# GroupNorm, attention and projection over 16 images: group statistics on VectorE, v's bias at v or at the attention's output, the accumulator as two tiles, and another place for raw projection weights

## The chip, the cores and the metric

The kernel runs on one core of a Trainium2 chip. The metric is the device time in microseconds (us) of one execution, given as the median of several runs. All times in this section of the document are of the kernel before the change.

## The reference

Sixteen images x of 512 channels and 32x32 positions (N = 1024), all in fp32, go through one layer:

```python
xg = x.reshape(b, NUM_GROUPS, -1)                    # 8 groups of 64 channels
mu = jnp.mean(xg, axis=-1, keepdims=True)
var = jnp.var(xg, axis=-1, keepdims=True)
xn = ((xg - mu) * jax.lax.rsqrt(var + EPS)).reshape(b, c, h, w)
xn = xn * norm_gamma[:, None, None] + norm_beta[:, None, None]
qkv = jnp.einsum('oc,bchw->bohw', qkv_w, xn) + qkv_b[:, None, None]
...
attn = jax.nn.softmax(jnp.einsum('bhnd,bhmd->bhnm', q, k) * scale, axis=-1)
out = jnp.einsum('bhnm,bhmd->bhnd', attn, v)         # 4 heads of 128 channels
...
out = jnp.einsum('oc,bchw->bohw', proj_w, out) + proj_b[:, None, None]
return x + out
```

As the softmax's weights of a position sum to one, v's bias may be added to v, or to the attention's output behind the division, or be carried through proj_w into the projection's bias.

## The kernel before

Channels lie in the 128 partitions, so an image is four tiles of 128x1024 (c = 0 to 3), and a group of 64 channels is half the partitions of one tile. The attention sets the pace. One step s is (image b, head h, key block j of 8); 512 steps make the run. In each step and for each half of 512 query positions PE (TensorE) computes scores s (`scores`, L844), ACT (ScalarE) the exp into p (L850), and PE, one step later, adds v times p to the accumulator po (`weighted_sum`, L912). DVE (VectorE) keeps the running sum of the exps, tot (L858), from which `denominators` and `divide` make the division. At j = 7 ACT copies po to the head's output o (L919).

All other work is cut into units that are dealt out into these steps by `plan_head` (L1059), and run between the two halves' attention matmuls (`run`, L1237). In head 0 an image makes q and k of its own heads 2 and 3; in head 1 the projection of the image before, and loading, statistics and normalising of the next; in head 2 the next image's q and k of heads 0 and 1; in head 3 its v (`v_groups`, L754). In image 0 the weights are prepared as well.

The three projections are two-level fast products of seven (`two_levels`, with the matmuls at L604): each inner product sums in PSUM (tags x and y of ps_a, two banks each); ACT copies partial results (L484), DVE adds them (L628), and the outer sums follow on DVE (L677). The weights' sums are made once in image 0 on DVE from raw blocks that SP's DMA queue loads (`stage_blocks` L367, `group_weights` L390), stored in DRAM (kept, L441) and later loaded from there (L406). For v, `finish` (L758) adds two outer parts (vt, L766), transposes in blocks (vu, L769) and sends the result through DRAM (L777, L782).

Statistics: `stats_chunk` (L256) lets ACT sum x and the squared deviations of each channel, for each of the four tiles. `stats_group` (L270) then averages over the channels of a group with two matmuls against avg, a matrix of 1/64: pm (L83) of the means and pv (L88) of the variances, with small DVE operations at L82 to L89, a power on POOL (GpSimd, L90), and sc, t, sh (L76, L100, L102). `normalise` (L293) applies scale and shift, mostly on ACT. In image 0's own opening the same steps are written out by hand.

v's bias: `bias_of_v` (L929), in head 1 of image 0, multiplies it with proj_w by 32 matmuls of one column (pb, L935; 4x4 blocks, fp32 matmuls are recorded twice) and adds it to the projection's bias.

The order on each engine is set by a scheduler that follows the order of the program. `tc.high_priority(URGENT)` lets an instruction go ahead of others of its engine, `tc.issue_after(ins)` puts one behind another, and `keep_in_program_order` pins it. The scheduler adds the semaphores. A matmul that overwrites a tile waits for the readers of that tile. po is one tile of two banks, [128, 1024]:

```python
if j == 0 and half == 0:
    po[b, h] = ps_o.tile([P, N], F32, tag="o", name=f"po_{b}_{h}")
...
last_eviction[b] = nc.scalar.copy(os_[b, h][:, i], po[b, h][:, i])
```

Of the kernel before, what the change touches and what calls it, by code (L numbers as in the profile page):

```python
# [186 lines left out]
def fast_path(ctx, tc, x, sources, out, consts, flag, dims):  # L187
# [35 lines left out]
    ones = one.tile([BLK, 1], F32, name="ones")  # L223
    xs, xb, vs, qs, ks, os_, ob = {}, {}, {}, {}, {}, {}, {}
# [23 lines left out]
    nc.vector.memset(neghalf, -0.5)  # L248
    for t, src in (
        (gamma_sb, gamma), (beta_sb, beta), (qkb_sb, qk_b), (vb_sb, v_b), (projb_sb, proj_b)  # L250
    ):
        nc.gpsimd.dma_start(t, src)
# [3 lines left out]
    def stats_chunk(b, c):  # L256
        if c == 0:
            mvs[b] = gn.tile([P, NCC, 2], F32, tag="mv", name=f"mv_{b}")

        junk = lpool.tile([P, N], F32, tag="tt", name=f"junk_{b}_{c}")  # L260
        sums = gn.tile([P, 3], F32, tag="st", name=f"sums_{b}_{c}")
        nc.scalar.activation(junk, xs[b, c], AF.Identity, accum_out=sums[:, 0:1])
        nc.scalar.mul(mvs[b][:, c, 0:1], sums[:, 0:1], 1.0 / N)
        nc.scalar.mul(sums[:, 1:2], sums[:, 0:1], -1.0 / N)
        nc.scalar.activation(
            junk, xs[b, c], AF.Square, bias=sums[:, 1:2], accum_out=sums[:, 2:3]
        )
        nc.scalar.mul(mvs[b][:, c, 1:2], sums[:, 2:3], 1.0 / N)

    def stats_group(b):  # L270


        g = []

        def part(n, first, last):
            if not g:
                g.extend(norm.group_steps(mvs[b]))
            with tc.issue_after(added[b - 1, 1, n].ins), tc.high_priority(URGENT):
                for step in g[first:last]:
                    step()  # L280

        def scale():
            n = 4 if b > 1 else 3
            part(n, 9, 10)
            with tc.issue_after(added[b - 1, 1, n].ins), tc.high_priority(URGENT):
                mu, sc = norm.result
                sh = norm.shift(mu, sc)
            for c in range(NCC):
                scaled[b, c] = sc, sh, c

        return [lambda: part(2, 0, 6), lambda: part(3, 6, 9), scale]
# [75 lines left out]
    def stage_blocks(site):  # L367
# [4 lines left out]
        if site in ("proj", "v"):  # L372
# [381 lines left out]
    def v_groups(b):  # L754
# [3 lines left out]
        def finish(which, h, a, c):  # L758
# [7 lines left out]
            nc.vector.tensor_add(t, a, c)  # L766
# [74 lines left out]
    def scores(s, half):  # L841
# [7 lines left out]
        with tc.high_priority(URGENT):  # L849
            exps[s] = nc.scalar.activation(ps[s][:, ts(half, HALF)], sc, AF.Exp, scale=SCALE)  # L850
        i = ts(half, HALF) if s == steps - 1 else ds(0, N)
# [55 lines left out]
    def weighted_sum(s, half):  # L907
        b, h, j = where(s)
        if j == 0 and half == 0:
            po[b, h] = ps_o.tile([P, N], F32, tag="o", name=f"po_{b}_{h}")  # L910
        i = ts(half, HALF)
        nc.tensor.matmul(  # L912
            po[b, h][:, i], v_block(b, h, j), ps[s][:, i],
            start=(j == 0), stop=(j == NB - 1),
        )
        if j == NB - 1:
            if (b, h) not in os_:
                os_[b, h] = opool.tile([P, N], F32, tag="o", name=f"o_{b}_{h}")
            last_eviction[b] = nc.scalar.copy(os_[b, h][:, i], po[b, h][:, i])  # L919

    def divide(b, h):
        nc.vector.tensor_mul(os_[b, h], os_[b, h], rinv.pop((b, h)))

# [4 lines left out]

    def bias_of_v(o):  # L929

        acc = ps_a.tile([P, HALF], F32, tag="y", name=f"pb_{o}")
        half, r = divmod(o, 2)
        for c in range(NCC):
            block = stage["proj"][f"a{half + 1}{c // KC + 1}"]
            nc.tensor.matmul(  # L935
                acc[:, 0:1], block[:, ts(r * KC + c % KC, P)], vb_sb[:, c : c + 1],
                start=(c == 0), stop=(c == NCC - 1),
            )
        nc.vector.tensor_add(
            projb_sb[:, o : o + 1], projb_sb[:, o : o + 1], acc[:, 0:1]  # L940
        )
# [116 lines left out]

    def plan_head(b, h):  # L1059
# [9 lines left out]
        elif h == 1:  # L1069
# [4 lines left out]
            else:  # L1074
                plan[0].append(lambda: load_x(b + 1))
                spread(plan, [lambda c=c: stats_chunk(b + 1, c) for c in range(NCC)], 2, 4)
                sums, power, scale = stats_group(b + 1)
                if b == 0:

                    plan[4] += [sums, power, scale]  # L1080
                else:
                    plan[4].insert(0, sums)
                    plan[4].insert((len(plan[4]) + 1) // 2, power)
                    plan[5].insert(0, scale)
                for r in range(2):
                    plan[5 + r] += [

                        lambda c=c, half=half: normalise(b + 1, c, half, b > 0 or c % 2 == 1)
                        for c in range(KC * r, KC * r + KC) for half in range(NH2)
                    ]  # L1090
                plan[6].append(lambda: x_sums(b + 1, (1,)))
            if b == 0:
                for g in range(len(OUTER)):
                    plan[g // 2].append(lambda g=g: kept_group("v", g))
                    plan[NB // 2 - 1 + g].append(lambda g=g: kept_group("proj", g))
                plan[2].append(lambda: stage_blocks("proj"))
                spread(plan, [lambda o=o: bias_of_v(o) for o in range(NCC)], 3, 5)
# [111 lines left out]

    plan = []  # L1210
    for s in range(steps + 1):
# [12 lines left out]
        for half in range(NH2):  # L1224
            if s < steps:
# [4 lines left out]
                if half == 1 and j == 4 and s > NB:  # L1230

                    with tc.issue_after(added[b, h, 4].ins):
                        divide(*where(s - NB)[:2])
            if s > 0:
                weighted_sum(s - 1, half)
            n = (len(units) + 1) // 2
            run(units[half * n : (half + 1) * n])  # L1237
        if s > 0:
            del ps[s - 1]
# [7 lines left out]
def general_path(ctx, tc, x, sources, out, consts, dims):  # L1247
# [26 lines left out]
    with tc.For_i(0, B, 1) as b:  # L1274
# [16 lines left out]
        for h in range(HEADS):  # L1291
# [9 lines left out]
            for qb in range(NB):  # L1301
# [27 lines left out]
                nc.scalar.copy(o[h][:, ts(qb, P)], acc[:, :P])  # L1329
# [46 lines left out]
```

## Time and profile before

| what | value |
|---|---|
| median of 3 runs | 3169.19 us (3167.69 to 3172.65) |
| profiled execution, its own time | 3171.08 us |
| its span | 3169.3 us |
| granted TensorE clock | 1.0 |
| mean DMA rate | 166 GB/s |
| L83 pm, 34 records | 4.9 us busy |
| L88 pv, 34 records | 6.5 us busy |
| L935 pb, 32 records | 3.8 us busy |
| L766 vt, 120 instructions | 90 of them 711 ns mean, 30 of them 712 |

How to read it. Times in the timeline count from the span's start. A row gives the start, the length, the engine, the line of the kernel, the operation, output <- inputs, tile shape and, behind x, the number of instructions joined in the row; in brackets stand idle time ahead of it and what ended it. Matmuls are pipelined: a row's length runs past the start of the next, so that the distance from start to start is what an instruction takes of PE. "PEld" is the loading of weights into PE, and "SPq" the DMA queue of SP. "Idle" in a group's row is the idle time of that engine just before its instructions.

### The profile page before, as it was taken

Reading aid. Unit: us, or ns where it says so; the run is one execution under the profiler, and the core shown is the slowest. Engines: PE = TensorE matmul, PEld = TensorE weight load, DVE = VectorE, ACT = ScalarE, POOL = GpSimd, SP = SyncE. Lnnn points to the kernel's source line nnn. Section 1 sums busy time; section 2 is a strip of 40 time slices with the busy share of each in tenths; the row PEclk is TensorE's granted clock in tenths of the full one; section 3 lists DMA queues with packets and bytes.
Section 4 is the critical chain, followed back from the end, with each engine's and each line's share of the span. In section 5 each row is a group of like instructions: output and inputs, shape, how many; then the busy total and the mean of one; then the engine's idle time right before and its main releaser. Section 6 shows DMA issues by size and latency. Waiting matters only on the chain.

```text
span 3169.3 us, 34227 instructions
## 1 busy us (share of the span) xinstructions
PE 3156.8 (100%) x10502; PEld 2188.2 (69%) x10502; DVE 2635.8 (83%) x4642; ACT 1438.3 (45%) x2711; POOL 516.3 (16%) x896
## 2 busy tenths in 40 slices
PE   9999999999999999999999999999999999999999
PEld 7566676677776776767767667677676776766664
DVE  9878879788897888878888787987879978788785
ACT  3535435354353443535435454453534545344333
POOL 0011221111211112211122111222012221122200
PEclk9999999999999999999999999999999999999999
DMA  5554554545545555454554545555455564555531
GB/s 176 186 190 154 187 173 152 173 152 194 168 164 163 155 184 176 167 165 144 193 173 159 170 144 192 167 174 171 144 177 170 176 187 133 178 158 187 180 119 48
DMA packets 210668, 524.83 MB, mean 166 GB/s; under 512 B 32176, under 2 KB 65456, under 8 KB 210480
## 3 DMA queue, kind: packets, MB, share of 16 engines
q1 hardware_dynamic: 133088, 282.39, 28.6%
q0 software_dynamic: 64000, 204.54, 19.3%
q10 hardware_dynamic: 13392, 35.66, 3.5%
q8 instruction: 86, 1.41, 0.2%
q14 instruction: 102, 0.84, 0.1%
HBM read 389.30 MB, written 133.17 MB: 165 GB/s over the span
## 4 chain that ended last, share of the span: by engine, by line
PE 96%; DVE 2%; DMA 1%; issue 0%; SPq 0%; POOL 0%; ACT 0%; ACTq 0%; DVEq 0%
PE s L844 27%; PE po L912 27%; PE qk_x L604 12%; PE qk_y L604 9%; PE pp_x L604 6%; PE v_x L604 6%; PE v_y L604 4%; PE pp_y L604 4%; PE lx L999 0%; DVE qk_t L572 0%; DMA x<-in_x 0%; PE ly L999 0%; DVE tot L858 0%; DVE qk_r L628 0%; DVE qk L712 0%
## 5 line engine op out<-in xcount | busy, mean ns | idle before, releaser
L912 PE MATMUL po<-p,v 128*128 128x512 f32 x2048 | 1049.4, 594 | 0.7 <-ACT p L850 0.7
L850 ACT ACTIVATE p<-s 128x512 f32<-128x512 f32 x1024 | 610.6, 596 | 963.7 <-PE s L844 960.0
L844 PE MATMUL s<-qk,qk 128*128 128x512 f32 x2048 | 1047.4, 593 | 0.3 <-DVE qk L712 0.3
L912 PEld LDWEIGHTS po<-p,v 128*128 128x128 f32 x2048 | 603.6, 302 | 322.7 <-issue 214.5
L858 DVE TENSOR_TENSOR tot<-tot,p 128x1024 f32<-128x1024 f32 x385 | 470.2, 1221 | 158.1 <-ACT p L850 156.1
L844 PEld LDWEIGHTS s<-qk,qk 128*128 128x128 f32 x2048 | 387.7, 190 | 88.6 <-issue 29.9
L604 PEld LDWEIGHTS qk_x<-qk_t,w 128*128 128x128 f32 x1344 | 251.8, 190 | 166.1 <-issue 75.3
L604 PE MATMUL qk_x<-qk_t,w 128*128 128x256 f32 x1344 | 356.3, 382 | 0.1
L484 ACT COPY qk_u<-qk_x 128x512 f32<-128x512 f32 (+1 forms) x256 | 136.2, 532 | 229.6 <-PE qk_x L604 229.6
L777 POOL DMA_DIRECT2D vd<-vu x120 | 66.6, 556 | 902.9 <-DVE vu L769 899.5
L628 DVE TENSOR_TENSOR qk_r<-qk_y,qk_u 128x512 f32<-128x512 f32 (+1 forms) x256 | 158.1, 618 | 34.7 <-ACT qk_u L484 21.5
L578 POOL DMA_DIRECT2D kept_t<-qk_t x240 | 129.3, 540 | 278.5 <-DVE qk_t L572 212.0
L604 PEld LDWEIGHTS pp_x<-pp_t,w_proj 128*128 128x128 f32 x630 | 117.2, 190 | 74.7 <-issue 32.3
L628 DVE TENSOR_TENSOR v_r<-v_y,v_u 128x512 f32<-128x512 f32 (+1 forms) x120 | 76.6, 638 | 110.5 <-ACT v_u L484 80.3
L604 PE MATMUL pp_x<-pp_t,w_proj 128*128 128x256 f32 x630 | 167.8, 383 | 0.0
L782 POOL DMA_DIRECT2D v<-vd x240 | 140.5, 592 | 166.6 <-DMA vd<-vu 63.3
L604 PE MATMUL v_x<-v_t,w_v 128*128 128x256 f32 x630 | 166.6, 381 | 0.0
L828 POOL DMA_DIRECT2D out_y<-y x120 | 65.9, 550 | 603.3 <-DVE y L827 601.5
L604 PEld LDWEIGHTS v_x<-v_t,w_v 128*128 128x128 f32 x630 | 118.4, 190 | 55.3 <-issue 19.1
L604 PE MATMUL qk_y<-x,w 128*128 128x256 f32 x512 | 142.2, 379 | 1.5 <-DVE qk_r L628 1.5
L769 DVE STREAM_TRANSPOSE vu<-vt 128x512 f32<-128x512 f32 x120 | 135.7, 1131 | 4.5 <-DMA vd<-vu 4.4
L712 DVE SCALAR_TENSOR_TENSOR qk<-qk_r,qkb_sb,qk_r 128x512 f32<-128x512 f32 x192 | 137.7, 744 | 1.6
(203 smaller groups left out, 4420.0 us busy)
## 6 DMA issues: line engine op xcount, KB each, us to landing
w<-kept SPq DMA_DIRECT2D x90, 512.0 KB, 3.7
kept_t<-qk_t POOLq DMA_DIRECT2D x180, 256.0 KB, 3.5
v_t<-kept_t SPq DMA_DIRECT2D x180, 256.0 KB, 2.9
w<-kept SPq DMA_DIRECT2D x90, 384.0 KB, 3.3
rinv<-row ACTq DMA_DIRECT2D x63, 512.0 KB, 5.0
x<-in_x POOLq DMA_DIRECT2D x60, 512.0 KB, 4.6
vd<-vu POOLq DMA_DIRECT2D x120, 256.0 KB, 3.0
v<-vd POOLq DMA_DIRECT2D x240, 128.0 KB, 4.2
```

Source lines behind the costliest of these rows:

```text
L484: nc.scalar.copy(t[n][:, :width], t["x"][:, :width])
L578: nc.gpsimd.dma_start(t, to)
L604: nc.tensor.matmul(acc[:, ts(i, Q)], have["w"][t][:, i, slot, :], inner(i, bn), start=(first and i == 0), stop=True, skip_group_check=True,)
L628: nc.vector.tensor_add(dst, view(a), view(c))
L712: nc.vector.scalar_tensor_tensor(st[b, h][:, ts(half, HALF)], a, qkb_sb[:, i : i + 1], c, ALU.add, ALU.add)
L769: nc.vector.transpose(u.rearrange("p (q i j) -> p j q i", q=n, i=BLK), t.rearrange("p (j q i) -> p j q i", q=n, i=BLK),)
L777: nc.gpsimd.dma_start(rows[which][ts(h, P), :], u)
L782: nc.gpsimd.dma_start(vs[b, pair][ts(q, BLK), half].rearrange("m h (k i) j -> m (h k) (i j)", k=n), rows[which].rearrange("(k m) (q e) -> ...
L844: nc.tensor.matmul(sc, ks[b, h][:, ts(j, P)], qs[b, h][:, ts(half, HALF)], start=True, stop=True)
L850: exps[s] = nc.scalar.activation(ps[s][:, ts(half, HALF)], sc, AF.Exp, scale=SCALE)
L858: added[b, h, j] = nc.vector.tensor_add(tot[b, h][:, i], tot[b, h][:, i], ps[s][:, i])
L912: nc.tensor.matmul(po[b, h][:, i], v_block(b, h, j), ps[s][:, i], start=(j == 0), stop=(j == NB - 1),)
```

## The change

Four things.

1. *Statistics of images 1 to 15.* ACT writes each tile's means and sums of squared deviations into the columns of a table of [128, 2, 32], which POOL sets to zero once (one small ACT multiplication a tile less). DVE sets the counts, transposes the table in 32x32 blocks, copies each quadrant's block beside that of its neighbour (32 partitions each), and one bn_aggr joins the 64 triples of count, mean and sum. POOL's power follows, on one column; then DVE transposes a broadcast of the result back, and makes sc, t and sh. The first part (`gather`) is issued behind the running sum of j = 3 in step 4, the second (`scale`) behind that of j = 4 in step 5 (in image 0: both in step 4, behind j = 3). No matmul is left; the opening of image 0 keeps its two pairs.
2. *v's bias.* `bias_of_v`'s matmuls go. From image 1 on the add at vt is a scalar_tensor_tensor that adds the bias too. Image 0's v comes out of another path and stays without it; there ACT adds the bias to each head's output, four activations of 128x1024, behind the exps of steps 18, 26, 34 and 38. The general path, which does not run here, adds it at its copy.
3. *po* is two tiles, one for each half.
4. *Image 0's head 1.* The raw blocks of proj_w and their sums lie in the tiles r0 and r1, which otherwise hold outer results, and are loaded in step 0 (before: in tiles of y and ot2, in step 2); the kept sums of proj are made one step earlier; image 1's odd tiles are normalised behind an exp. In images 1 to 14 the running sum of head 1, j = 6 is issued behind the units of its step.

```diff
@@ -223,2 +223,3 @@
     ones = one.tile([BLK, 1], F32, name="ones")
+    table = one.tile([P, 2, BLK], F32, name="table")
     xs, xb, vs, qs, ks, os_, ob = {}, {}, {}, {}, {}, {}, {}
@@ -248,2 +249,3 @@
     nc.vector.memset(neghalf, -0.5)
+    nc.gpsimd.memset(table, 0.0)
     for t, src in (
@@ -256,5 +258,6 @@
     def stats_chunk(b, c):
-        if c == 0:
-            mvs[b] = gn.tile([P, NCC, 2], F32, tag="mv", name=f"mv_{b}")
+        mean, spread_ = (
+            (mvs[b][:, c, 0:1], mvs[b][:, c, 1:2]) if b == 0
+            else (table[:, 0, c : c + 1], table[:, 1, c : c + 1])
+        )
         junk = lpool.tile([P, N], F32, tag="tt", name=f"junk_{b}_{c}")
@@ -262,8 +265,10 @@
         nc.scalar.activation(junk, xs[b, c], AF.Identity, accum_out=sums[:, 0:1])
-        nc.scalar.mul(mvs[b][:, c, 0:1], sums[:, 0:1], 1.0 / N)
+        nc.scalar.mul(mean, sums[:, 0:1], 1.0 / N)
         nc.scalar.mul(sums[:, 1:2], sums[:, 0:1], -1.0 / N)
         nc.scalar.activation(
-            junk, xs[b, c], AF.Square, bias=sums[:, 1:2], accum_out=sums[:, 2:3]
+            junk, xs[b, c], AF.Square, bias=sums[:, 1:2],
+            accum_out=sums[:, 2:3] if b == 0 else spread_,
         )
-        nc.scalar.mul(mvs[b][:, c, 1:2], sums[:, 2:3], 1.0 / N)
+        if b == 0:
+            nc.scalar.mul(spread_, sums[:, 2:3], 1.0 / N)
@@ -272,17 +277,26 @@
-        g = []
+        v = nc.vector
+        quads = P // BLK
+        k = slice(0, NCC)
+        t = {}
-        def part(n, first, last):
-            if not g:
-                g.extend(norm.group_steps(mvs[b]))
-            with tc.issue_after(added[b - 1, 1, n].ins), tc.high_priority(URGENT):
-                for step in g[first:last]:
-                    step()
+        def gather():
+            t["all"] = lpool.tile([P, N], F32, tag="tt", name=f"groups_{b}")
+            rows = t["all"][:, : 6 * BLK].rearrange("p (s j) -> p s j", s=3)
+            both = t["both"] = t["all"][:, 6 * BLK : 6 * BLK + 2]
+            ve = t["all"][:, 6 * BLK + 2 : 6 * BLK + 3]
+            v.memset(rows[:, 0, :], float(N))
+            v.transpose(rows[:, 1:3, :BLK], table)
+            for q in range(quads):
+                v.tensor_copy(rows[ts(q, BLK), 1:3, BLK:], rows[ts(q ^ 1, BLK), 1:3, :BLK])
+            v.bn_aggr(both, rows.rearrange("p s j -> p j s"))
+            v.tensor_scalar_add(ve, both[:, 1:2], EPS)
+            nc.gpsimd.tensor_tensor(both[:, 1:2], ve, neghalf[:, 0:1], ALU.pow)
         def scale():
-            n = 4 if b > 1 else 3
-            part(n, 9, 10)
-            with tc.issue_after(added[b - 1, 1, n].ins), tc.high_priority(URGENT):
-                mu, sc = norm.result
-                sh = norm.shift(mu, sc)
+            back = t["all"][:, 8 * BLK : 10 * BLK].rearrange("p (s j) -> p s j", s=2)
+            v.transpose(back, t["both"].unsqueeze(2).to_broadcast([P, 2, BLK]))
+            sc = gn.tile([P, NCC], F32, tag="sc", name="sc")
+            v.tensor_mul(sc, back[:, 1, k], gamma_sb)
+            sh = norm.shift(back[:, 0, k], sc)
             for c in range(NCC):
@@ -290,3 +304,7 @@
-        return [lambda: part(2, 0, 6), lambda: part(3, 6, 9), scale]
+        def part(n, step):
+            with tc.issue_after(added[b - 1, 1, n].ins), tc.high_priority(URGENT):
+                step()
+        return [lambda: part(3, gather), lambda: part(4 if b > 1 else 3, scale)]
@@ -371,3 +389,10 @@
         names = ("a11", "a12", "a21", "a22", "s1", "s2")
-        if site in ("proj", "v"):
+        if site == "proj":
+            r = [
+                rpool.tile([P, 2, 2, HALF], F32, tag=f"r{i}", name=f"st_{site}_{i}")
+                for i in range(2)
+            ]
+            for i, n in enumerate(names):
+                st[n] = r[i // 4][:, i // 2 % 2, i % 2, :]
+        elif site == "v":
             for n in names[:4]:
@@ -765,3 +790,4 @@
             t = ypool.tile([P, HALF], F32, tag="y", name=f"vt_{b}_{pair}_{h}_{half}")
-            nc.vector.tensor_add(t, a, c)
+            i = 2 * pair + h
+            nc.vector.scalar_tensor_tensor(t, a, vb_sb[:, i : i + 1], c, ALU.add, ALU.add)
@@ -850,2 +876,7 @@
             exps[s] = nc.scalar.activation(ps[s][:, ts(half, HALF)], sc, AF.Exp, scale=SCALE)
+        if not (h == 1 and j == 6 and 0 < b < B - 1):
+            running_sum(s, half)
+    def running_sum(s, half):
+        b, h, j = where(s)
         i = ts(half, HALF) if s == steps - 1 else ds(0, N)
@@ -908,7 +939,7 @@
         b, h, j = where(s)
-        if j == 0 and half == 0:
-            po[b, h] = ps_o.tile([P, N], F32, tag="o", name=f"po_{b}_{h}")
+        if j == 0:
+            po[half] = ps_o.tile([P, HALF], F32, tag=f"o{half}", name=f"po_{b}_{h}_{half}")
         i = ts(half, HALF)
         nc.tensor.matmul(
-            po[b, h][:, i], v_block(b, h, j), ps[s][:, i],
+            po[half], v_block(b, h, j), ps[s][:, i],
             start=(j == 0), stop=(j == NB - 1),
@@ -918,3 +949,3 @@
                 os_[b, h] = opool.tile([P, N], F32, tag="o", name=f"o_{b}_{h}")
-            last_eviction[b] = nc.scalar.copy(os_[b, h][:, i], po[b, h][:, i])
+            last_eviction[b] = nc.scalar.copy(os_[b, h][:, i], po[half])
@@ -923,2 +954,5 @@
+    def bias_of_v(b, h):
+        nc.scalar.activation(os_[b, h], os_[b, h], AF.Identity, bias=vb_sb[:, h : h + 1])
     def spread(plan, units, first, last):
@@ -928,16 +962,2 @@
-    def bias_of_v(o):
-        acc = ps_a.tile([P, HALF], F32, tag="y", name=f"pb_{o}")
-        half, r = divmod(o, 2)
-        for c in range(NCC):
-            block = stage["proj"][f"a{half + 1}{c // KC + 1}"]
-            nc.tensor.matmul(
-                acc[:, 0:1], block[:, ts(r * KC + c % KC, P)], vb_sb[:, c : c + 1],
-                start=(c == 0), stop=(c == NCC - 1),
-            )
-        nc.vector.tensor_add(
-            projb_sb[:, o : o + 1], projb_sb[:, o : o + 1], acc[:, 0:1]
-        )
     def kept_group(site, g):
@@ -1058,2 +1078,6 @@
+    def behind_exp(unit):
+        with tc.issue_after(exps[max(exps)].ins):
+            unit()
     def plan_head(b, h):
@@ -1076,16 +1100,20 @@
                 spread(plan, [lambda c=c: stats_chunk(b + 1, c) for c in range(NCC)], 2, 4)
-                sums, power, scale = stats_group(b + 1)
+                gather, scale = stats_group(b + 1)
                 if b == 0:
-                    plan[4] += [sums, power, scale]
+                    plan[4] += [gather, scale]
                 else:
-                    plan[4].insert(0, sums)
-                    plan[4].insert((len(plan[4]) + 1) // 2, power)
+                    plan[4].insert(0, gather)
                     plan[5].insert(0, scale)
                 for r in range(2):
-                    plan[5 + r] += [
-                        lambda c=c, half=half: normalise(b + 1, c, half, b > 0 or c % 2 == 1)
-                        for c in range(KC * r, KC * r + KC) for half in range(NH2)
+                    units = [
+                        [lambda c=c, half=half: normalise(b + 1, c, half, b > 0 or c % 2 == 1)
+                         for half in range(NH2)]
+                        for c in range(KC * r, KC * r + KC)
                     ]
+                    if b > 0:
+                        plan[5 + r] += units[0] + units[1]
+                    else:
+                        plan[5 + r] += units[0]
+                        for at, u in zip((0, NB), units[1]):
+                            plan[6 + r].insert(at, lambda u=u: behind_exp(u))
                 plan[6].append(lambda: x_sums(b + 1, (1,)))
@@ -1094,5 +1122,4 @@
                     plan[g // 2].append(lambda g=g: kept_group("v", g))
-                    plan[NB // 2 - 1 + g].append(lambda g=g: kept_group("proj", g))
-                plan[2].append(lambda: stage_blocks("proj"))
-                spread(plan, [lambda o=o: bias_of_v(o) for o in range(NCC)], 3, 5)
+                    plan[NB // 2 - 2 + g].append(lambda g=g: kept_group("proj", g))
+                plan[0].insert(0, lambda: stage_blocks("proj"))
         elif b + 1 == B:
@@ -1209,2 +1236,5 @@
+    biased = {(h + 2) * NB + 2: h for h in range(HEADS - 1)}
+    biased[HEADS * NB + 6] = HEADS - 1
     plan = []
@@ -1233,2 +1263,6 @@
                         divide(*where(s - NB)[:2])
+                if half == 1 and s in biased:
+                    with tc.issue_after(exps[s].ins):
+                        bias_of_v(0, biased[s])
             if s > 0:
@@ -1237,2 +1271,4 @@
             run(units[half * n : (half + 1) * n])
+        if s < steps and h == 1 and j == 6 and 0 < b < B - 1:
+            running_sum(s, 1)
         if s > 0:
@@ -1328,3 +1364,5 @@
                     )
-                nc.scalar.copy(o[h][:, ts(qb, P)], acc[:, :P])
+                nc.scalar.activation(
+                    o[h][:, ts(qb, P)], acc[:, :P], AF.Identity, bias=vb_sb[:, h : h + 1]
+                )
         for i in range(NCC):
```

## The prediction

> **What bounds the kernel now.** First the busy times at the head of the page, then the chain that ended last:
>
> ```profile
> PE 3156.8 (100%) x10502; PEld 2188.2 (69%) x10502; DVE 2635.8 (83%) x4642; ACT 1438.3 (45%) x2711; POOL 516.3 (16%) x896
> ...
> PE 96%; DVE 2%; DMA 1%; issue 0%; SPq 0%; POOL 0%; ACT 0%; ACTq 0%; DVEq 0%
> ```
>
> TensorE (PE) is busy from end to end and carries 96% of the chain. So a matmul taken away shortens the run, and a wait on VectorE (DVE) costs only where PE really stands. Busy shares can't price small matmuls, since matmuls are pipelined. I read start-to-start distances in the timeline: 429 ns for every matmul of 512 columns, 215 for 256; what exceeds that is a bubble. All bubbles together are some 43 us of 3169, so no change of this kind can win more.
>
> Next the timeline where the statistics stand in a usual image:
>
> ```profile
> 2857.17 0.28 PE L83 MATMUL pm<-mean,avg 128*128 128x4 f32 x2
> 2857.31 1.11 PE L604 MATMUL pp_x<-ot,w_proj 128*128 128x256 f32 x4
> 2858.25 1.02 PE L844 MATMUL s<-qk,qk 128*128 128x512 f32 x2
> 2859.11 1.03 PE L604 MATMUL pp_x<-pp_t,w_proj 128*128 128x256 f32 x4
> ...
> 2864.38 0.38 PE L88 MATMUL pv<-vv,avg 128*128 128x4 f32 x2
> 2864.62 1.10 PE L844 MATMUL s<-qk,qk 128*128 128x512 f32 x2
> 2865.56 1.02 PE L912 MATMUL po<-p,v 128*128 128x512 f32 x2
> ```
>
> Two or four records on one row must advance the start column by 0.86 us: s to pp_x does (2858.25 to 2859.11). The four pp_x after pm take 0.94 (2857.31 to 2858.25), and the two s after pv 0.94 (2864.62 to 2865.56): the neighbours pay too. Then the same two matmuls and pb in image 0:
>
> ```profile
> 122.31 1.84 PE L935 MATMUL pb<-vb_sb,st_a 128*128 128x1 f32 x16
> 124.02 1.10 PE L844 MATMUL s<-qk,qk 128*128 128x512 f32 x2
> ...
> 132.35 0.39 PE L83 MATMUL pm<-mean,avg 128*128 128x4 f32 x2 [1.22 <-DVE mean L82]
> ```
>
> Here PE stands: the two po matmuls from 130.11 have their turn until 130.97, pm starts at 132.35.
>
> **The change part by part.**
>
> *Statistics off PE, 14 usual images.* pm: 28 ns before it, 112 for its own weights (avg is loaded, not v or w), 84 at the s behind it: 0.224 us. pv: 85 + 132 + 112 + 84 = 0.413 us. Together 0.637 us, times 14 = **8.9 us gained**. The Trainium skill, page "TensorE: Matmul & The Clock Gate", section "Back-to-back issue gap", prices a matmul of few columns at a floor of about 60 cycles, some 25 ns. By that alone, four records an image would give an estimated 0.1 us, 1.4 us in all. The rows speak against so small a gain, as they show the exposed weight load and the neighbours' loss.
>
> *The same work on VectorE, at no cost.* Removed are copy, subtract, multiply, add, copy, add: rows of 150 to 163 ns that advance the queue by 72 to 117, some 0.6 us. Added are a memset, a block transpose of 128x64, four copies of 32x64, a bn_aggr over 64 triples, an add, and after POOL's pow a transpose back. The trace has none of these shapes. From below each advances the queue like a 128x4 row (72 ns), from above like the 128x256 add (0.33 us). Nearest are the 32x32 transpose L875 (194 ns, advancing about 128) and the small rows; I take about 1.4 us for all, 0.8 more than before. They go behind the running sum of j=3 (in the timeline of one image 1489.47) and j=4 (1496.49). Behind the first, two pp_t and y wait, and then DVE idles 1.19 us (until 1493.16, for PE). The next PE matmul that waits for a DVE result there, pp_y at 1502.93, has 1.14 us to spare. So 0.8 us is covered; without that cover each image would pay up to 0.8 us, 11 us in all. ACT loses four small multiplications an image and is 45% busy: nothing. POOL's pow stays, on one column.
>
> *Image 1's statistics, made in image 0.* 1.38 us of idle at pm and 0.33 + 0.33 for the two matmuls with their neighbours: **2.0 us gained**.
>
> *pb.* Sixteen records before 124.02 cost 1.79 us; the rest of the 32, in two places (134.72 to 135.62, 136.56 to 137.37), 0.98 and 0.89: **3.7 us gained**. In place of it ACT adds the bias to image 0's four outputs, four activations of 128x1024. The nearest rows, ACT's other passes of that size, take 1.04 to 1.14 us. Each stands behind an exp, and the next exp behind it; matmuls that wait for these have about 1.8 us to spare. Bounds 0 and 1 us each; I take 0.
>
> *v's bias elsewhere: the vt add becomes scalar_tensor_tensor, 120 times.*
>
> ```profile
> L712 DVE SCALAR_TENSOR_TENSOR qk<-qk_r,qkb_sb,qk_r 128x512 f32<-128x512 f32 x192 | 137.7, 744 | 1.6
> ...
> L766 DVE TENSOR_TENSOR vt<-v_r,v_r 128x512 f32<-128x512 f32 x90 | 64.0, 711 | 0.5
> ```
>
> Start to start the add advances DVE by 600 ns and the L712 form by 663: 63 ns more each. Who waits? In the v stage:
>
> ```profile
> 1409.74 0.74 DVE L766 TENSOR_TENSOR vt<-v_r,v_r 128x512 f32<-128x512 f32 x1
> ...
> 1410.66 0.48 DVE L628 TENSOR_TENSOR v_r<-v_y,v_p 128x256 f32<-128x256 f32 x1
> ...
> 1411.52 0.70 PE L604 MATMUL v_y<-x,w_v 128*128 128x256 f32 x2
> ```
>
> v_y at 1411.52 starts 55 to 76 ns behind the end of the second v_r, in all 15 images: PE is released by DVE here. DVE is without a gap from 1394.4 on, and four vt stand in that stretch ahead of it (1395.13, 1397.81, 1407.86, 1409.74). 4 x 63 = 0.25 us an image, times 15 = **3.8 us lost**. After this stretch every PE wait on DVE has at least 1.06 us to spare, so the other four vt cost nothing. The bounds are 0 (the matmul waits for something else as well) and all eight, 0.50 x 15 = 7.6 us; I take four, since only these stand ahead. The Trainium skill, page "VectorE: DVE Perf Modes", section "The TRN2 errata — SBUF-src ops pay a fixed extra latency per instruction", gives (N+151)/0.96 ns for an add of two fp32 operands, 691 ns at N = 512. The adds agree (684 to 690 in quieter stretches), L712's 744 does not: the third operand costs. By that formula alone the loss would be 0 and the forecast 3.8 us lower.
>
> *po as two tiles.* With one tile the first matmul of one half waits for ACT's copy of the other half. Where nothing else of PE lies between, this shows: four times 84 ns in image 0 (from 110.99) and five times 206 ns in image 15 (from 3083.66), **1.4 us gained**. Elsewhere the wait ends 0.94 us or more ahead: 0.
>
> *Image 0's staging, sooner, and what is late next.* PE comes 5.7 us earlier to the second half of image 0. Three things may then be late. (1) sh of image 1 and ACT's normalise of x: before, pow at 135.32 and sh at 137.32; with the shorter chain I estimate sh near 133.9, about when PE can bear it; bounds 0 and 3.6 us. (2) the first weights of the next group. The DMA engines are near full from 146 to 162, and a load of 512 KB takes 4.9 us there:
>
> ```profile
> 148.71 0.32 SPq L406 DMA_DIRECT2D w<-kept  x1
> ...
> 159.21 0.67 PE L604 MATMUL qk_x<-x,w 128*128 128x256 f32 x2 [0.64 <-DMA w<-kept]
> ```
>
> SP's queue takes them in order behind the kept sums' stores, which move up by a step only. PE uses the load of 148.71 at 153.93 (qk_x), 5.2 us later, and would now want it 5.7 sooner; I estimate it 1 us late, since the stores ahead of it move up too. The stall at 159.21 (0.8 us now) may grow by 0.7 in the same way. (3) the raw blocks, now loaded at step 0 of this head: seven us from issue to use, about in time. I take 1.0 + 0.7 + 0.8 = **2.5 us lost**; bounds 0 and all 5.7. Elsewhere SP's queue isn't touched. The running sum of j=6 moved behind the units of its step is a reordering within DVE: 0.
>
> **The sum.** 8.9 + 2.0 + 3.7 + 1.4 - 3.8 - 2.5 = 9.7 us. Against the profiled execution, 3171.08 (span 3169.3 and 1.8 around it), that gives 3161.4; this execution is 1.9 above the median of the three runs, so on the median 3169.19 it is **3159.5 us**.
>
> **The rivals.**
>
> *R1, DVE absorbs vt and image 0 hides its waits.* No loss: 16.0 us, 3153.2. For it: the v_y wait is only some 60 ns long. Against: no idle of DVE lies in that stretch.
>
> *R2, image 0 gives back all it won,* because x and w set its end: 8.9 + 1.4 - 3.8 = 6.5 us, 3162.7; with a further 2 us of DMA collisions (two such stalls exist already, 0.8 at 159.21 and 1.5 at 2998.9) 3164.7. For it: full DMA engines. Against: part of the idle at pm was DVE's chain, now shorter.
>
> *R3, the gather becomes the bound.* It is urgent on DVE behind the sum of j=3, and pp_t, y and pp_r wait behind it. Of 1.14 us to spare 0.8 is taken, so it decides from 1.75 us for gather and scale together (1.4 + 0.34); each us beyond costs 14 us in all. At 2.4 us the gain is gone (9.7/14 = 0.7 beyond), at 2.9 the kernel is slower by 0.2%: 3175.5. For it: nine dependent instructions of unseen shape. Against: all nine would have to take the 0.33 us of a 128x256 add to reach 2.9.
>
> *R4, the small matmuls leave but their time doesn't,* since PE then stands for the pp_r results that they filled (pv starts 56 ns behind one): only half of the 8.9: 5.2 us, 3164. Against: the next pp_y have 1.1 to 4.4 us to spare.
>
> In a sentence by itself: the Trainium skill, page "SBUF — State Buffer", section "Who interferes with whom", has DVE and POOL exclude each other at a shared port; no row here lets me price that for the one pow an image.
>
> **Chances.** Forecast 0.50 (3156.5 to 3162), R1 0.14, R2 0.20, R3 0.08, R4 0.08. About 0.2%, 6.3 us, is what a measurement of this kernel can tell from no change: faster is below 3162.9. The forecast and R1 are faster (0.64) and half of R2 (0.10): 0.74. Same: the rest of R2 and R4, 0.18. Slower: R3, 0.08. The range runs from R1 to the far end of R2 and R4: 3153 to 3166.
>
> **What would show it.** No L83 or L88 in the steady timeline, and pp_x and s 0.86 us apart there; an image's period 195.8 - 0.64 + 0.25 = 195.4 us. The vt row at about 744 ns, and v_y still 55 to 76 ns behind v_r, 0.25 us later. In image 0 a DMA w or ACT x as the releaser of PE. The forecast is wrong if v_y's excess grows by more than 0.5 us, if a pp_y waits for DVE in h=1, or if image 0's h=2 begins less than 1 us or more than 5.7 us sooner.

## The result

The changed kernel takes 3160.56 us (median of 9 runs, 3159.32 to 3162.20), the kernel before 3169.19 (9 runs, 3167.60 to 3172.65): a ratio of 0.9973, 95% interval 0.9965 to 0.9982. It is 8.6 us faster; forecast were 9.7 (3159.5, range 3153 to 3166). The profiled execution took 3162.20 us with a span of 3160.4.

The head of its page, and its chain:

```profile
PE 3146.9 (100%) x10410; PEld 2176.9 (69%) x10410; DVE 2658.2 (84%) x4683; ACT 1437.4 (45%) x2655; POOL 496.2 (16%) x897
...
PE 96%; DVE 2%; DMA 1%; issue 0%; SPq 0%; ACT 0%; ACTq 0%; POOL 0%; DVEq 0%; POOLq 0%
```

PE has 92 records fewer (60 of the statistics, 32 of pb) and is still busy from end to end; DVE has 22 us more to do. PE's bubbles (what start-to-start distances have above 429, 215 and 112 ns) fell from 43.3 to 34.9 us. The timeline of PE where the statistics stood, in the same image as before:

```profile
2850.10 1.03 PE L629 MATMUL pp_x<-pp_t,w_proj 128*128 128x256 f32 x4
2850.96 1.03 PE L629 MATMUL pp_x<-ot,w_proj 128*128 128x256 f32 x4
2851.82 1.02 PE L870 MATMUL s<-qk,qk 128*128 128x512 f32 x2
2852.68 1.03 PE L629 MATMUL pp_x<-pp_t,w_proj 128*128 128x256 f32 x4
```

Every row starts 0.86 us behind the last. The account is taken from the start of each head's first s in both traces (32 records of s make a head). Head 1 is 0.557 us shorter in the mean of the images 1 to 14, the rest of an image 0.08 to 0.17 longer from image 2 on (image 1: 0.13 shorter), and image 0, from head 1 to head 3, takes 82.78 us in place of 83.24.

What the gather takes of DVE, in the image that the prediction read:

```profile
1487.57 0.78 DVE L291 COPY groups<-groups 32x64 f32<-32x64 f32 x4
1488.38 0.42 DVE L597 TENSOR_TENSOR pp_t<-ot,pp_t 128x256 f32<-128x256 f32 x1
1488.72 1.01 DVE L292 BATCH_NORM_AGGREGATE groups<-groups 128x2 f32<-128x192 f32 x1
1489.65 0.63 DVE L853 TENSOR_TENSOR y<-y,pp_r 128x512 f32<-128x512 f32 x1
```

From start to start the four copies take 0.81 us and bn_aggr 0.93. The next PE matmul that waits for DVE, the pp_y of which the prediction said that it had 1.14 us to spare, first in the kernel before and then in the changed one:

```profile
1501.12 0.68 DVE L628 TENSOR_TENSOR pp_r<-pp_y,pp_u 128x512 f32<-128x512 f32 x1
1502.93 1.03 PE L604 MATMUL pp_y<-ot,w_proj 128*128 128x256 f32 x4
...
1498.07 0.68 DVE L653 TENSOR_TENSOR pp_r<-pp_y,pp_u 128x512 f32<-128x512 f32 x1
1498.90 1.03 PE L629 MATMUL pp_y<-ot,w_proj 128*128 128x256 f32 x4
```

The distance from the end of pp_r to pp_y falls from 1.14 to 0.15 us. A matmul that is really late for DVE starts some 55 ns behind it in these traces (v_y below, pp_y in E7 and E8), so 0.1 us is left. PE doesn't stand here.

The v stage, by the rows that answer to those of before:

```profile
1404.40 0.82 DVE L792 SCALAR_TENSOR_TENSOR vt<-v_r,vb_sb,v_r 128x512 f32<-128x512 f32 x1
1405.06 0.50 DVE L597 TENSOR_TENSOR qk_t<-qk_t,x 128x256 f32<-128x256 f32 x1
1405.39 1.16 DVE L795 STREAM_TRANSPOSE vu<-vt 128x512 f32<-128x512 f32 x1
...
1406.34 0.74 DVE L792 SCALAR_TENSOR_TENSOR vt<-v_r,vb_sb,v_r 128x512 f32<-128x512 f32 x1
...
1406.95 0.46 DVE L597 TENSOR_TENSOR qk_t<-x,qk_t 128x256 f32<-128x256 f32 x1
...
1407.61 0.47 DVE L653 TENSOR_TENSOR v_r<-v_y,v_u 128x256 f32<-128x256 f32 x1
...
1408.13 0.70 PE L629 MATMUL v_y<-x,w_v 128*128 128x256 f32 x2
```

The first vt advances DVE by 660 ns, the second, behind a transpose, by 610. v_y stands 55 ns behind v_r as before, now 0.135 us later than PE could have started it. And image 0:

```profile
136.08 0.15 DVE L102 TENSOR_TENSOR sh<-beta_sb,t 128x4 f32<-128x4 f32 x1
...
136.27 1.52 ACT L109 ACTIVATE x<-x,sh,sc 128x512 f32<-128x512 f32 x2 [4.09 <-DVE sh L102]
...
137.69 0.57 ACT L876 ACTIVATE p<-s 128x512 f32<-128x512 f32 x1
...
138.32 1.77 PE L870 MATMUL s<-qk,qk 128*128 128x512 f32 x2 [2.48 <-ACT p L876]
...
148.28 2.25 SPq L431 DMA_DIRECT2D w<-kept  x4
...
154.52 1.10 PE L629 MATMUL qk_x<-x,w 128*128 128x256 f32 x4 [1.36 <-DMA w<-kept]
```

ACT stands 4.09 us for sh with a normalisation at the head of its queue; the exp behind it is late, and with it PE, which stands 2.6 us. From 138.66 to 142.07 the granted TensorE clock is 0.5, where it is 1.0 before and behind: each matmul of 512 columns takes 853 ns there in place of 429, and that costs PE 1.8 us more. Then PE stands 1.5 us for the next weights. Most of what image 0 had won is gone.

### The profile page after: what moved, and what is told of

It is laid out like the page before. It is cut to its first block, busy times and chain, and to the rows that moved or that the text cites. A ratio compares the mean times of both kernels' runs of the same rounds, so it can differ in the third digit from the quotient of the medians.

```text
span 3160.4 us, 34006 instructions
## 1 busy us (share of the span) xinstructions
PE 3146.9 (100%) x10410; PEld 2176.9 (69%) x10410; DVE 2658.2 (84%) x4683; ACT 1437.4 (45%) x2655; POOL 496.2 (16%) x897
## 4 chain that ended last, share of the span: by engine, by line
PE 96%; DVE 2%; DMA 1%; issue 0%; SPq 0%; ACT 0%; ACTq 0%; POOL 0%; DVEq 0%; POOLq 0%
PE po L943 27%; PE s L870 27%; PE qk_x L629 12%; PE qk_y L629 9%; PE pp_x L629 6%; PE v_x L629 6%; PE v_y L629 4%; PE pp_y L629 4%; PE lx L1019 0%; DVE qk_t L597 0%; DMA x<-in_x 0%; PE ly L1019 0%; DMA w_v<-in_qkv_wT 0%; DMA w<-kept 0%; DVE qk L737 0%
## 5 line engine op out<-in xcount | busy, mean ns | idle before, releaser
L509 ACT COPY qk_u<-qk_x 128x512 f32<-128x512 f32 (+1 forms) x256 | 136.2, 532 | 230.0 <-PE qk_x L629 230.0
```

The lines of the kernel that those rows point to most:

```text
L509: nc.scalar.copy(t[n][:, :width], t["x"][:, :width])
```

## The experiments

Three or four kernels at a time ran on one chip beside runs of the kernel before (medians there 3168.5 to 3169.0). "Changed" is 3160.56, and 3160.04 in its second sample (E10). The ratios' intervals reach some 0.1%, 3 us, to either side: what is smaller than that rests on the traces and not on the medians.

**E1, vt without the bias**

```diff
-            nc.vector.scalar_tensor_tensor(t, a, vb_sb[:, i : i + 1], c, ALU.add, ALU.add)
+            nc.vector.tensor_add(t, a, c)
```

> The changed kernel with vt a plain addition of two operands again, so that v's bias is left out from image 1 on. Theory A (from the trace after): the longer form costs DVE 60 ns only where the instruction before it is not a block transpose, which holds for two of the four vt ahead of v_y; v_y is 0.13 us late in each image, and all 15 images give back 1.9 us: 3158.7 us against 3160.6, v_y at 0.105 us of excess instead of 0.24. Theory B (the prediction's size): four vt of 63 ns, 3.8 us: 3156.8. Theory C: the wait is not from vt at all, 0: 3160.6.

3159.65 us (7 runs, ratio 0.9969, 0.9958 to 0.9980). The medians lie too close to separate 1.9 from 0 or 3.8; the traces do it. By the starts of the heads this kernel wins 0.12 us on the changed one in head 3 of image 0 and 1.75 more from there to the end, 0.08 to 0.18 in head 3 of each image: theory A's size. (In heads 1 and 2 of image 0 it wins another 1.5, which is the half clock of the changed kernel's trace and not vt.) The starts of the vt in head 3 show why: behind a transpose vu the long form advances DVE by 593 to 615 ns (median 598), as the plain addition did (592 to 621, median 599), behind anything else of the stretch ahead of v_y by 661 to 669 (before 602 to 611). What in the transpose covers it, no run here shows.

**E2, statistics on TensorE again**: `stats_chunk` and `stats_group` of before, and in `plan_head`

```diff
-                gather, scale = stats_group(b + 1)
+                sums, power, scale = stats_group(b + 1)
...
-                    plan[4].insert(0, gather)
+                    plan[4].insert(0, sums)
+                    plan[4].insert((len(plan[4]) + 1) // 2, power)
```

> The changed kernel with the statistics of images 1 to 15 made as before, by two matmuls on TensorE each, and everything else as changed. Theory A: each of 14 images loses 0.56 us again (0.64 for the matmuls, less 0.08 for a wait of pp_x for ACT that stands in their place now), 7.8 us; image 1's part costs less than its 2.0, as PE waits there for the image's scale and weights anyway: 3168.4 to 3170.4 us. Theory B: the matmuls' places are filled by waits for DVE's gather, so that little is lost: under 4 us, below 3164.6.

3167.98 us (11 runs, ratio to before 0.9997, 0.9988 to 1.0006): putting them back costs 7.4 to 7.9 us, nearly the whole gain. Head 1 is longer by 0.55 to 0.56 us in each of the images 1 to 14, 7.8 us in all. Theory A holds, 0.4 us below its range; B falls.

**E3, po as one tile**

```diff
-            po[half] = ps_o.tile([P, HALF], F32, tag=f"o{half}", name=f"po_{b}_{h}_{half}")
+            po[b, h] = ps_o.tile([P, N], F32, tag="o", name=f"po_{b}_{h}")
```

> The changed kernel with po as one tile of two banks again. Theory A: the five waits of 0.206 us in image 15 return (1.0 us), the four of 0.084 in image 0 return but are hidden in the wait for the next weights: 3161.6 us. Theory B: two tiles do nothing for the end, 0: 3160.6. Theory C: both return in full, 1.4: 3162.0.

3162.11 us (11 runs, 0.9977, 0.9968 to 0.9986). From the last image's head 2 on it loses 0.83 us to the last s against the changed kernel, which is four waits of 0.206; a fifth follows the last s. In image 0 waits of 84 to 86 ns are back (at 111.28, 113.08 and 142.25), but PE's waits for sh and w follow there. A, as far as the trace goes; the medians can't tell 1.0 from 1.4.

**E8, the running sum at its old place**, in head 1, j = 6 of the images 1 to 14

```diff
-        if not (h == 1 and j == 6 and 0 < b < B - 1):
-            running_sum(s, half)
+        running_sum(s, half)
...
-        if s < steps and h == 1 and j == 6 and 0 < b < B - 1:
-            running_sum(s, 1)
```

> The changed kernel with the running sum of head 1, j = 6 at its old place ahead of the units of its step, in images 1 to 14. On DVE it changes places with a sum of x's halves. Theory A (the prediction): a reordering within DVE that no PE wait depends on, within 0.5 us: 3160.6. Theory B: DVE has about 0.1 us to spare at pp_y in this head now, the sum's 1.14 us come in front of what PE waits for, and the loss is up to 1 us an image: up to 3174.

3165.41 us (11 runs, 0.9987, 0.9978 to 0.9996): 4.9 us lost, where the prediction had said 0. By the starts of the heads it loses 0.31 to 0.32 us in head 1 of each of the images 1 to 14, 4.3 us in all. The timeline of the kernel with the sum at its old place, DVE and PE, shows where:

```profile
1509.65 1.22 DVE L888 TENSOR_TENSOR tot<-tot,p 128x1024 f32<-128x1024 f32 x1
...
1510.79 0.42 DVE L653 TENSOR_TENSOR pp_r<-pp_y,pp_u 128x256 f32<-128x256 f32 x1
...
1511.26 0.70 PE L629 MATMUL pp_y<-o,w_proj 128*128 128x256 f32 x2
```

The last pp_r of the head stands right behind a running sum, and pp_y 54 ns behind the end of pp_r: it is 0.21 us late, and the matmul behind it another 0.1. In the changed kernel the same pp_y has 388 ns. Theory B. This is not the pp_y of the prediction's 1.14 us but one 10.6 us later; the former has 0.15 us in this kernel too. And the old place in the program is not the old place on DVE. In the kernel before the sum came behind that pp_r:

```profile
1511.81 0.42 DVE L628 TENSOR_TENSOR pp_r<-pp_y,pp_u 128x256 f32<-128x256 f32 x1
...
1512.74 1.22 DVE L858 TENSOR_TENSOR tot<-tot,p 128x1024 f32<-128x1024 f32 x1
```

So with the change's other edits the sum would have come ahead of the pp_r, and the moved line keeps it behind.

**E7, bn_aggr twice**

```diff
+            v.bn_aggr(t["all"][:, 10 * BLK : 10 * BLK + 2], rows.rearrange("p s j -> p j s"))
             v.bn_aggr(both, rows.rearrange("p s j -> p j s"))
```

> The changed kernel with the bn_aggr of 64 triples made twice in images 1 to 15 (the first result is not used), 0.93 us more on DVE in the gather. Theory A (the third rival of the prediction, with the cover as the trace after shows it: pp_y has 0.1 us to spare near the end of head 1): DVE's delay reaches PE almost whole, 0.3 to 0.85 us in each of 14 images, 4 to 12 us: 3165 to 3172.5. Theory B: DVE's idle time in head 1 takes it up, under 1 us in all: 3160.6 to 3161.6.

3175.02 us (11 runs, 1.0018, 1.0009 to 1.0027): 14.5 us lost, slower than before. Head 1 grows by 0.90 us in each of 14 images (12.6), and image 0, from head 1 to head 3, by 1.5, most of it at half clock (see below). The row in head 1:

```profile
1507.11 1.13 PE L630 MATMUL pp_y<-ot,w_proj 128*128 128x256 f32 x4 [0.62 <-DVE pp_r L654]
```

The second bn_aggr advances DVE by 0.88 us. pp_y, 54 ns behind the end of pp_r now, is 0.78 us late: 0.1 was covered. The matmul behind a wait takes 0.1 us more, here as in E8, and so 0.90 reach PE. Theory A, a little beyond its upper end.

**E4, image 1 normalised later**

```diff
-                        for at, u in zip((0, NB), units[1]):
-                            plan[6 + r].insert(at, lambda u=u: behind_exp(u))
+                        moved = [lambda u=u: behind_exp(u) for u in units[1]]
+                        if r == 0:
+                            plan[7] += moved
+                        else:
+                            late["x1"] = moved + [lambda: x_sums(b + 1, (1,))]
...
```

(`late["x1"]` goes to the front of the next head's step 0.)

> The changed kernel with image 1's odd tiles normalised later: tile 1 at the end of step 15 and tile 3 at the start of step 16, each behind an exp that is already there, so that no exp waits on ACT behind a normalisation that waits for sh. Theory A (image 0's end is set by proj's weight sums on DVE, their stores and the load of the next weights behind them): PE's wait of 1.0 to 2.6 us near 135 goes, the wait of qk_x for w near 150 grows by as much, and the total moves by less than 0.8 us: 3159.8 to 3161.4. Theory B (the late sh sets it): 1.0 to 4 us are won, 3156.5 to 3159.5.

3161.80 us (9 runs, 0.9976, 0.9966 to 0.9985): nothing won. PE's wait near 135 is gone, head 2 starts at 135.51 (138.32 and 137.09 in the two samples of the changed kernel), and the wait of qk_x is 3.39 us (from 148.39 to 151.77) in place of 1.52 and 2.67. So 0.8 to 1.0 us of waiting is saved in all. But the granted clock is 0.5 from 151.15 to 154.57, which costs the matmuls behind the wait 1.5 us. Theory A by the place and the total; the half clock is no part of it.

**E5, eight of proj's sums on POOL**

```diff
+        eng = nc.gpsimd if site == "proj" and g > 1 else nc.vector
...
```

(The four sums behind it go to `eng`.)

> The changed kernel with eight sums of proj's last two weight groups, in image 0, on POOL instead of DVE. DVE is free of 3 us there, and the next weights' load stands behind POOL's sums. Theory A (sums, stores and the load set image 0's end): the time moves with the moment at which the last store is issued (144.4 to 148.2 now): sooner if POOL needs less than 4 us for them, then up to 2.5 us are won, 3158 to 3160; later if it needs more, and then each us is lost. Theory B (sh and ACT set it): no change beyond 0.5 us, wherever the store ends up.

3170.20 us (11 runs, 1.0002, 0.9993 to 1.0012): 9.6 us lost, in image 0.

```profile
141.02 5.86 POOL L462 TENSOR_TENSOR w_proj<-w_proj 128x128 f32<-128x128 f32 x1 [7.93 <-DVE w_proj L455]
146.96 0.46 POOL L463 TENSOR_TENSOR w_proj<-w_proj,w_proj 128x128 f32<-128x128 f32 x1
...
152.28 4.82 SPq L431 DMA_DIRECT2D w<-kept  x4
...
158.27 2.04 PE L630 MATMUL qk_x<-x,w 128*128 128x256 f32 x4 [10.19 <-DMA w<-kept]
```

POOL's eight sums end some 10 us after their inputs, the stores wait for them, the load of w stands behind the stores in SP's queue, and PE stands 10 us for w. Theory A's other side; B is refuted.

**E6, both edits**

> The changed kernel with both edits: normalisations later, and the eight sums on POOL. Theory A: both waits shrink together, if POOL isn't slower than DVE was: 2.5 to 4.5 us won, 3156 to 3158; if it is slower, the time is that of the kernel with the sums on POOL alone, within 0.8 us. Theory B: the time is that of the kernel with the later normalisations alone.

3168.34 us (11 runs, 0.9999, 0.9990 to 1.0008): PE's wait for w is 9.9 us. It is 1.9 below E5, more than the 0.8 that theory A left, but within the intervals; by the starts of the heads, from head 1 to head 3 of image 0, it is 0.9 below.

**E9, pb put back**: `bias_of_v` of before as `pb_of_v`, beside the new additions

```diff
+                spread(plan, [lambda o=o: pb_of_v(o) for o in range(NCC)], 3, 5)
```

> The changed kernel with the 32 matmuls pb and their four additions put back into image 0, while ACT's and vt's additions of v's bias stay, so that the bias is counted twice. Theory A (the next weights set image 0's end, PE's own work there is covered): the 3.7 us of pb are taken out of PE's waits for sh and w, and the time is that of the changed kernel within 1 us. Theory B (as the prediction priced it): 2 us or more are lost.

3161.42 us (11 runs, 0.9977, 0.9968 to 0.9986): 0.9 and 1.4 above the two samples of the changed kernel (the latter ran on the same chip), between A and B by the medians. In the trace pb takes 3.6 us of PE again (16 records from 122.25, 16 from 127.47). The wait for sh shrinks to 0.06, qk_x waits for w 1.7 us (until 152.58), and a later load costs 1.4 (at 162.83). So pb is covered in part, some 60% by the median on the same chip. The traces don't fix it closer: from head 1 to head 3 of image 0 it takes 83.4 us here, 82.8 and 81.0 in the two of the changed kernel.

**E10, the changed kernel again**

> The changed kernel itself, as a second sample beside the others: 3160.6 us within 1; PE's two waits in image 0 (sh near 135, w near 150) come to 4.5 to 6.5 us together, moving with the moment at which SP issues the raw loads of proj_w (125 to 127 in the runs so far), and no wait of PE in image 15's head 0, if the 1.65 us of the run before were a chance of that execution.

3160.04 us (8 runs, 0.9974, 0.9964 to 0.9985). Waits in image 0 of 1.7 us at sh and 2.7 at w, and none in image 15:

```profile
137.09 1.12 PE L870 MATMUL s<-qk,qk 128*128 128x512 f32 x2 [1.55 <-ACT p L876]
147.05 2.26 SPq L431 DMA_DIRECT2D w<-kept  x4
152.73 1.10 PE L629 MATMUL qk_x<-x,w 128*128 128x256 f32 x4 [2.50 <-DMA w<-kept]
```

**E11, the eight sums left out**

```diff
+        if site == "proj" and g > 1:
+            nc.scalar.copy(w[0][:, :n, 2:4, :].rearrange("p n m d -> p n (m d)"),
+                           w[0][:, :n, 0:2, :].rearrange("p n m d -> p n (m d)"))
+            nc.scalar.copy(at("s4"), at("a22"))
+        else:
...
```

> The changed kernel with the eight sums of proj's last two weight groups left out; ACT copies blocks in their place, in four copies, so the projection's weights are wrong in part. Theory A (sums, stores and the load set image 0's end): the last store leaves SP 1 to 3 us sooner than at 13.5 us behind the raw loads, the load of w and qk_x come as much sooner, and up to 2.5 us are won: 3158 to 3159.5. Theory B (sh and ACT's normalisation set it, or the DMA engines' load does): within 0.7 us of the changed kernel.

3159.14 us (7 runs, 0.9971, 0.9959 to 0.9982), 0.9 and 1.4 below the changed kernel. The load of w is issued at 143.95 and qk_x starts at 149.22 after a wait of 0.6 us; a wait of 1.1 us follows at 152.6. Theory A has the direction and the place; the size is at the edge of what the medians tell.

What sets image 0's end can be read from these traces in one column, the distance from SP's issue of proj's raw loads to its issue of the first load of w. The last three columns hold PE's longest wait between head 1 and head 3, the most that PE stood there within one slot of 3.41 us (see below the table), and how long the granted clock was 0.5, with what this cost PE's matmuls:

| kernel | raw loads | w | distance | qk_x | longest wait | in one slot | half clock, cost |
|---|---|---|---|---|---|---|---|
| changed | 126.67 | 148.28 | 21.6 | 154.52 | 2.6 | 2.64 | 3.4, 1.8 |
| E10, the same | 125.42 | 147.05 | 21.6 | 152.73 | 2.7 | 1.82 | none |
| E1 (same code in image 0) | 125.21 | 146.94 | 21.7 | 152.83 | 2.9 | 2.05 | none |
| E8 (same code in image 0) | 125.44 | 147.17 | 21.7 | 152.88 | 2.7 | 2.76 | 3.4, 1.7 |
| E4, x later | 125.00 | 146.32 | 21.3 | 151.77 | 3.4 | 2.77 | 3.4, 1.5 |
| E9, pb back | 125.80 | 147.53 | 21.7 | 152.58 | 1.7 | 1.78 | none |
| E11, sums left out | 125.70 | 143.95 | 18.3 | 149.22 | 1.4 | 1.47 | none |
| E5, sums on POOL | 125.01 | 152.28 | 27.3 | 158.27 | 10.4 | 3.41 | 10.2, 2.0 |

PE's work ahead of it (E9) and ACT's order (E4) don't move the distance by more than 0.4 us; the sums do, both ways.

The half clock is a second price of a long wait. In all 13 traces here the granted clock, once it is up at the run's start, changes only at whole multiples of 3.41 us from that moment. At the end of eight such slots it was halved (E2, E3, E6 and E7 have one each too), and in each of these PE had stood 2.26 us or more; where it had stood 2.05 us or less in a slot at full clock, the clock stayed. So a wait of 2.7 us costs 1.7 us more when it falls into one slot (E8), and nothing when a slot's end divides it (E10: 1.36 and 1.30).

## Why the prediction was right

The total was 1.1 us off. The terms, in its order:

- *Statistics off PE, 8.9 us: 7.8.* The mechanism and the 0.637 us are as read. 0.08 of it comes back: in the image of the rows above a pp_x at 2871.30 starts 83 ns behind the end of ACT's copy pp_p, and is 0.08 late; in the kernel before the same pp_x had no wait. E2 also decides between the rows' price and that of the Trainium skill, page "TensorE: Matmul & The Clock Gate", section "Back-to-back issue gap": 7.8 us, not 1.4.
- *The gather at no cost: so it came, but the sum behind it was wrong.* Gather and scale were to take 1.4 us of DVE; start to start they take 2.1, with 0.8 for the copies and 0.93 for bn_aggr. The row that was taken for them, a 32x32 transpose that advances DVE by 128 ns, was too cheap for the copies and no model for bn_aggr. By the third rival's own sum, which decides from 1.75, this should have cost 0.35 us in each of 14 images, 5 us. It cost nothing at that pp_y, since the cover was added up wrong twice. DVE's idle time behind the sum of j = 3, 1.36 us (1.19 and 0.17), is cover as well, and is gone in the changed trace. And PE comes 0.64 us sooner by the very gain of the statistics, which shortens the cover. What is left is 0.1 us; that the two errors cancel so nearly is luck. E7 shows the price beyond it: 0.90 us an image for 0.88. So the third rival was nearer than its 8%. The Trainium skill, page "VectorE: DVE Perf Modes", section "Two Vector instructions with no wait between them", gives a model in which an instruction whose operands start in other partition quarters than the last ones did is held until all before it are done. The copies agree: rows of 186 ns that advance the queue by 195 to 220, where the 128x4 rows of 150 to 163 advance it by 72 to 117.
- *The moved running sum, "a reordering within DVE: 0".* Here a step failed. At its old place in the program the sum comes ahead of the last pp_r of head 1, and PE pays 0.31 us an image, 4.3 us in all (E8). The forecast of no loss in head 1 held only through this edit.
- *vt, 3.8 us lost: 1.9* (0.08 to 0.18 an image by E1). The place and the releaser were right, the size was not: the 63 ns hold for two of the four vt, and the other two stand behind a transpose (E1). By the Trainium skill's formula for additions alone (page "VectorE: DVE Perf Modes", section "The TRN2 errata — SBUF-src ops pay a fixed extra latency per instruction") vt would have cost no more; 90 of its 120 rows went from 711 to 751 ns.
- *Image 0: 3.2 us net (5.7 won, 2.5 lost): 0.5 in the first trace, 2.3 in E10's.* The 1.8 between the two are the half clock of the first. The prediction's (1) failed in size: sh is there at 135.0 (E10) to 136.2, not near 133.9, and PE waits 1.7 and 2.6 us. (2) was near: 2.7 and 1.5 for w, against 1.7. But the two are one: E4 shows that what is saved at sh is mostly paid at w. The half clock behind a wait stood in no term of the prediction. Of 5.7 us won on PE ahead of qk_x 1.5 are left in the mean of four traces. The second rival described this half of the change; its time was not met, since vt cost half.
- *po: 1.4: 1.0 in image 15*, the 0.34 of image 0 being lost in its waits (E3).
- *The profiled execution.* The prediction took off the 1.9 us by which it lay above the median without a reason. Its trace has a wait of PE of 1.65 us at 2998.9 that none of the twelve other traces here has, and that may be most of it; one trace of the kernel before can't show that its other executions lack it. The prediction called this wait a DMA collision; the view names DVE's qk_r as what ended it. With the wait taken off, the starts of the last s differ by 7.6 us (9.2 with it), and by 9.7 in E10's trace.

The sum by what was measured: 7.8 - 1.9 + 1.5 (the mean of image 0 in four executions with the same code, two of them with the half clock: 81.7 us from head 1 to head 3 against 83.24) + 1.0 = 8.4, against 8.6 in the medians. So 3.2 us too much was counted as won (1.1 in the statistics, 1.7 in image 0, 0.4 at po) and 1.9 too much as lost; the total is nearer than its terms, and that is luck.

Open: where vt's 60 ns go behind a transpose, and why the raw loads' moment differs by 1.7 us between executions. The half clock may be the larger part of the runs' scatter, for it hangs on where a wait falls in a slot: of E10's eight runs four have a mean granted clock of 1.0 and take 3159.5 to 3160.0 us, four have 0.999 and take 3160.1 to 3162.1.

## What to carry to other kernels

Price small matmuls in a dense TensorE stream by what their neighbours pay, not by their own rows, and then ask what VectorE does with the work. Its cover is its idle time and the slack at the next wait together, less what TensorE itself gains: here 0.1 us of it was left, and one moved addition was worth half of the gain. An edit that "only reorders" is to be priced by the wait behind it after the other edits, not before them. Where a stage's end hangs on a chain of loads, sums and stores in one queue, time won on the busy engine ahead of it is handed to the next wait; and a wait of 2.3 us or more can cost 1.5 us on top, where the granted clock falls behind it.

## What was not expected of the hardware

- A bn_aggr over 64 triples (128x192 elements in) takes 1.01 us and advances VectorE by 0.93. In the kernel before a bn_aggr of 12 elements takes 0.21.
- The granted TensorE clock fell to 0.5 at the end of each slot of 3.41 us in which PE had stood 2.26 us or more, for one, two or three slots, and cost 1.5 to 3.1 us.
- POOL's first sum, of 128x128, took 5.86 us in E5, the seven that follow 0.46 to 0.73 each; in E6 the first, of 128x256, took 7.29. POOL's spans in a profile are rough, but the stores behind them waited as long. Why the first is slow isn't settled.
- A three-operand form that costs VectorE 60 ns more costs nothing directly behind a block transpose of 128x512.
